# Layer 0 of a graph-attention stack: rows that travel by rank with all they need, wider MAX8 chunks, biases on TensorE

## The chip, the cores and the metric

The kernel runs on one core of a Trainium2 chip. The metric is the device time of one execution in microseconds; lower is better. It took 3183.84 us, the median of three runs (3183.69 to 3191.36).

## The reference

Four graph-attention layers run over 3327 nodes of 256 features and one adjacency matrix that they share. It is symmetric, with a full diagonal; a row has about 32 neighbours besides itself, and 52 at the most. Each layer adds its result to its input and normalises the row. Only layer 0 matters here:

```python
g_src = nodes @ W_src_w.T + W_src_b
g_tgt = nodes @ W_tgt_w.T + W_tgt_b
g = leaky_relu(g_src[:, None, :] + g_tgt[None, :, :], 0.2)
score = einsum('ijc,c->ij', g, a_w)
score = where(adj_mat != 0, score, -inf)
x = layernorm(x + softmax(score, axis=1) @ g_tgt)
```

The leaky ReLU stands inside the sum over features, so a score needs work on all 256 features of each pair. With about 1% of the pairs present, the kernel does it for the neighbours alone.

## The kernel before

Rows lie in 26 tiles of 128 (the last has 127). `sparse0` computes layer 0; the rest, `layers`, computes layers 1 to 3 with dense masks. At the very end one number, `lost`, says whether the sparse way dropped a neighbour; then `dense0` and the layers would run again.

The tiles form three sets of 5, 9 and 12 (`SETS`). For each tile `neighbours` (on VectorE, DVE) does the following:

- It loads the tile's adjacency rows in two halves of 1664 columns (`adj_i`, two buffers, SP's queue) and turns each entry into a column number or zero (`num`, L417).
- MAX8 takes the eight largest numbers of each chunk of `CHUNK` columns (L436). The first three of each chunk, and the eight largest of all the others (L445), go into `few`.
- Seven rounds of MAX8 and MATCH_REPLACE over `few` (L448, L450) give a sorted list of up to `KMAX` = 56 neighbours, `found`.
- The list, the row's own number and a mark for the diagonal form the row's `payload`. The number of neighbours gives a sort key; `key_rows` (TensorE) and L490 turn the keys of the set into ranks (`ranks_i`, L494).

Rows of a set are then processed in the order of their ranks, those with most neighbours first, so that a tile of 128 rows gathers only as many columns of lists as its first row needs (`LEVELS`). For this the rows must be rearranged. `write_list` (GpSimd, POOL) scatters a tile's payloads by rank into `lists_d`; `read_lists` loads the whole set's lists in rank order (`lst`).

Beside this, for every tile, `targets` projects the rows by `w_tgt` on TensorE, adds the bias on DVE (L358), copies one column on ACT (L359) and writes the row to `table_d` and to `own_d`. `sources` does the same with `w_src`, adds and negates on DVE (L374) and writes to `own_d`. So a row of `own_d` (`OWN` = 772 words) holds the row's negated source, its input x (copied straight from DRAM on POOL's queue) and its target.

The main loop walks over 126 parts of up to eight list columns. For a part q:

- `gather(q + 4)` issues one indirect DMA on POOL per list column (`g`, L544): 128 rows of `table_d`. Before a tile's first part it gathers the tile's rows of `own_d` by their own numbers (`own_of`, L536).
- `score(q)` (DVE) takes the larger of target and negated source (L563) and sums it, weighted by `a_w` (L569).
- After a tile's last part, `combine` takes the softmax; ACT scales the gathered rows (L650) and TensorE adds them up (L653). `add_input` (DVE) adds x, and `put_back` (POOL) scatters the result to `sums_d`.

The steps of `neighbours` for sets two and three are spread over the parts by a fixed plan (`owed`, `goal`), so DVE alternates between scores of one set and lists of the next. List writes wait in `between` and are issued one per two gathers. The order on PE, DVE, ACT and POOL in `sparse0` is the order of the program; SP's order is made by the framework's scheduler. Waits on a queue hold everything that stands behind them.

Of the kernel before, what the change touches and what calls it, by code (L numbers as in the profile page):

```python
# [8 lines left out]
F32 = mybir.dt.float32  # L9
BF16 = mybir.dt.bfloat16  # L10
I32 = mybir.dt.int32
U32 = mybir.dt.uint32
U16 = mybir.dt.uint16
AF = mybir.ActivationFunctionType
ALU = mybir.AluOpType
AX = mybir.AxisListType
# [3 lines left out]
P = 128  # L20
# [7 lines left out]
KMAX = 56  # L28
CHUNK = 64
FIRST = 3  # L30


SETS = (5, 9, 12)
# [6 lines left out]
FAR = 1e6  # L40

ROW = 260
OWN = 772


@with_exitstack
def gat_stack(
# [54 lines left out]
    table_d = dram.tile([nt * P, ROW], F32, name="table_d")  # L102
# [161 lines left out]

    def sparse0(lost):
        GROUP, TURNS, LEAD = 8, 11, 4
        starts = [sum(SETS[:s]) for s in range(len(SETS))]
        with ExitStack() as s0:
# [14 lines left out]
            w_tgt = const0.tile([P, kc, dim + 1], F32, name="w_tgt0")  # L283
            nc.sync.dma_start(w_tgt[:, :, :dim], w_tgt_t.rearrange("(c p) f -> p c f", p=P))
            a_row = load_row(const0, a_w, "a_row")
            bt_row = load_row(const0, b_tgt, "bt_row")
            w_src = const0.tile([P, kc, dim], F32, name="w_src0")
            nc.scalar.dma_start(w_src, w_src_t.rearrange("(c p) f -> p c f", p=P))
            bs_row = load_row(const0, b_src, "bs_row")
# [12 lines left out]
            for lo, hi in halves:  # L302
                hi = -(-hi // P) * P
                rev_i = io0.tile([P, nt * P // 2], I32, tag="adj_i", name="rev_i")
                nc.gpsimd.iota(
                    rev_i[:, : hi - lo], pattern=[[-1, hi - lo]], base=n - lo,
                    channel_multiplier=0,
                )
                nc.vector.tensor_copy(rev[:, lo:hi], rev_i[:, : hi - lo])
# [14 lines left out]
            for s, size in enumerate(SETS):  # L324
                lo, hi = starts[s] * P, min(n, (starts[s] + size) * P)
                own_d.append(dram.tile([size * P, OWN], F32, name=f"own{s}_d"))
                copy_rows(nc.gpsimd, own_d[s][: hi - lo, dim : 2 * dim], x[lo:hi, :])
# [12 lines left out]
            def project(p, xt, pn, weight):  # L340
                for k in range(kc):
                    nc.tensor.matmul(
                        p[:pn, : weight.shape[2]], xt[:, k, :pn], weight[:, k, :],
                        start=(k == 0), stop=(k == kc - 1),
                    )

            def targets(it):

                xt, pn = columns_of(it)
                row = io0.tile([P, ROW], F32, tag="row", name="row", bufs=3)  # L350
                nc.vector.memset(row[:, dim:], 0.0)
                if pn < P:
                    nc.vector.memset(row[:, :dim], 0.0)
                    nc.vector.memset(row[:, dim : dim + 1], -FAR)
                pt = ps0.tile([P, BANK], F32, tag="acc", name="pt")
                project(pt, xt, pn, w_tgt)
                yield
                nc.vector.tensor_add(row[:pn, :dim], pt[:pn, :dim], bt_row[:pn])  # L358
                nc.scalar.copy(row[:pn, dim : dim + 1], pt[:pn, dim : dim + 1])  # L359
                nc.scalar.dma_start(table_d[it * P : (it + 1) * P, :], row)  # L360
                nc.scalar.dma_start(own_rows(it)[:, 2 * dim :], row)
                yield

            def sources(it):

                xt, pn = columns_of(it)
                pss = ps0.tile([P, BANK], F32, tag="ps", name="pss", bufs=1)
                project(pss, xt, pn, w_src)
                yield
                minus = io0.tile([P, dim], F32, tag="minus", name="minus")  # L370
                if pn < P:
                    nc.vector.memset(minus, 0.0)
                    nc.scalar.dma_start(own_rows(it)[pn:, dim : 2 * dim], minus[pn:])
                nc.vector.scalar_tensor_tensor(  # L374
                    minus[:pn], pss[:pn, :dim], -1.0, bs_row[:pn],
                    op0=ALU.mult, op1=ALU.subtract,
                )
                nc.scalar.dma_start(own_rows(it)[:, :dim], minus)
                yield

            lists_d = [
                dram.tile([size * P, KMAX + 2], U32, name=f"lists{s}_d")
# [5 lines left out]

            len_c = nt * P // CHUNK

            def neighbours(s):
# [6 lines left out]
                payloads = []  # L398
                of_rows = iter(())
                for t in range(size):  # L400
# [7 lines left out]
                    for b, (lo, hi) in enumerate(halves):  # L408
# [12 lines left out]
                        if lo <= it * P < hi:  # L421

                            at0 = it * P - lo
                            own_v = v[:, at0 : at0 + P]
                            junk = io0.tile([P, P], F32, tag="junk", name="junk")
                            nc.vector.scalar_tensor_tensor(
                                junk, own_v, -1.0, ident, op0=ALU.mult, op1=ALU.mult,
                                accum_out=sums[:, 2:3],
                            )
                            nc.vector.tensor_mul(own_v, own_v, off_diag)  # L430
                        chunks = padded // CHUNK
                        for c in range(chunks):
                            if c == chunks // 2:
                                next(of_rows if b else before, None)
                                yield
                            nc.vector.max(  # L436
                                cand[:, lo // CHUNK + c, :], v[:, c * CHUNK : (c + 1) * CHUNK]
                            )
                        yield
                    few = io0.tile([P, FIRST * len_c + 8], F32, tag="few", name="few")  # L440
# [4 lines left out]
                    nc.vector.max(few[:, FIRST * len_c :], cand[:, :, FIRST:])  # L445
                    found = io0.tile([P, KMAX], F32, tag="found", name="found")
                    for r in range(0, KMAX, 8):
# [11 lines left out]
                    payload = io0.tile([P, KMAX + 2], U32, tag=f"pay{t}", name="payload", bufs=1)  # L459
                    nc.vector.tensor_scalar(  # L460
                        payload[:, :KMAX], found, -1.0, float(n), op0=ALU.mult, op1=ALU.add
# [5 lines left out]
                    payloads.append(payload)  # L467
# [27 lines left out]
                placed[s] = ranks_i, payloads  # L495
# [5 lines left out]
            def write_list(s, t):  # L501
                ranks_i, payloads = placed[s]
                nc.gpsimd.indirect_dma_start(
                    out=lists_d[s][:, :],
                    out_offset=bass.IndirectOffsetOnAxis(ap=ranks_i[:, t : t + 1], axis=0),
                    in_=payloads[t][:, :], in_offset=None,
                )

            def read_lists(s):
                lst = io0.tile([P, max(SETS), KMAX + 2], U32, tag="lst", name="lst")  # L510
                nc.gpsimd.dma_start(
                    lst[:, : SETS[s], :], lists_d[s].rearrange("(t p) k -> p t k", p=P)
# [17 lines left out]
            def gather(q):  # L530
                (s, t), k0, k1 = parts[q]
                if k0 == 0:
# [3 lines left out]
                    nc.gpsimd.indirect_dma_start(  # L536
                        out=own[:, :], out_offset=None, in_=own_d[s][:, :],
                        in_offset=bass.IndirectOffsetOnAxis(ap=lst[:, KMAX : KMAX + 1], axis=0),
                    )
# [40 lines left out]
            def score(q):  # L580
# [6 lines left out]
                if k0 == 0:  # L587
                    sc = entry["sc"] = io0.tile([P, KMAX + 1], F32, tag="sc", name="sc", bufs=3)
                    if kt < KMAX:
                        at = nt + starts[s] + t  # L590
                        nc.vector.tensor_scalar(
                            lost[:, at : at + 1], entry["lst"][:, kt : kt + 1], float(n), None,
                            op0=ALU.is_lt,
# [206 lines left out]


# [44 lines left out]
            read_lists(0)  # L846

# [823 lines left out]
```

The softmax here doesn't subtract the row's maximum and nothing guards it: scores larger than these inputs give would overflow.

## Time and profile before

| | us |
|---|---|
| median of three runs | 3183.84 |
| profiled execution | 3182.83 |
| its span | 3181.0 |
| first adjacency tile arrives on DVE | 27.2 |
| ranks of the first set | 142.8 |
| first gather | 168.0 |
| last gather | 1514.9 |
| last result of layer 0 put back | 1540.8 |

In the profile, PE is TensorE, PEld its weight load, DVE VectorE, ACT ScalarE, POOL GpSimd and SP SyncE; L544 is line 544 of the kernel. A group of instructions is shown with its count, its busy time, the mean of one in ns, and the idle time of its engine just ahead of it. DVE is busy for 2316.7 us of the span (73%), PE for 2170.4 (68%), POOL for 1042.3 (33%), ACT for 734.7 (23%); these are means over stages with different limits. A line of a timeline gives start, duration, engine and instruction, and in brackets how long the engine stood idle ahead of it and what released it.

### The profile page before, as it was taken

To read this page: it belongs to the slowest core of one execution; us is meant where nothing else is said; L and a number is where in the kernel's file an instruction comes from. 1 tells how busy PE (TensorE), PEld (TensorE's weight loads), DVE (VectorE), ACT (ScalarE), POOL (GpSimd) and SP (SyncE) were. 2 spreads that over 40 slices of the span, in tenths; PEclk is the share of its full clock that TensorE was granted. 3 is DMA by queue.
4 is the path that set the end of the run, shared out by engine and by line. 5 is a ranking of instruction groups with operands and counts; after the bars stand their busy time and mean duration, and the time that the engine had idled before them with its cause. 6 is when DMAs were issued, how large, how long until landed. Compare 5 with 4: busy or idle time off the path is not lost.

```text
span 3181.0 us, 44618 instructions
## 1 busy us (share of the span) xinstructions
PE 2170.4 (68%) x15572; PEld 1239.5 (39%) x15572; DVE 2316.7 (73%) x6592; ACT 734.7 (23%) x2068; POOL 1042.3 (33%) x1056
## 2 busy tenths in 40 slices
PE   4204324335352445443689999999999999999996
PEld 2102112112121222221468888885444445444332
DVE  6879999999976655555425552107888898899997
ACT  0003222324331434433234431120111110110110
POOL 0077747677767777777100000000000000000000
PEclk6556666667676677666799999999999999999998
DMA  7556536655434544444657663332212212212211
GB/s 208 156 138 175 154 99 164 172 152 163 123 83 111 136 109 120 117 118 114 190 145 216 200 189 91 109 104 82 65 47 70 67 49 68 67 48 57 57 47 46
DMA packets 177752, 367.93 MB, mean 116 GB/s; under 512 B 34340, under 2 KB 123236, under 8 KB 176494
## 3 DMA queue, kind: packets, MB, share of 16 engines
q1 hardware_dynamic: 95798, 171.81, 19.3%
q0 software_dynamic: 51424, 157.02, 18.9%
q10 hardware_dynamic: 30296, 36.15, 3.2%
q8 instruction: 125, 2.05, 0.3%
q14 instruction: 109, 0.89, 0.1%
HBM read 322.84 MB, written 45.43 MB: 116 GB/s over the span
## 4 chain that ended last, share of the span: by engine, by line
PE 45%; DVE 4%; DMA 1%; issue 0%; ACT 0%; POOL 0%; ACTq 0%; SPq 0%; DVEq 0%; POOLq 0%
PE acc L1326 17%; PE acc L1279 15%; PE acc L1334 8%; DVE e L1195 3%; PE misc L1125 3%; DMA at_i<-in_adj_t_dram 1%; DMA at<-at_d 1%; PE misc L1222 0%; PE misc L1408 0%; PE misc L1369 0%; DVE h L246 0%; DVE stats L1486 0%; DVE h L1484 0%; DVE h L1299 0%; DVE both L1481 0%
## 5 line engine op out<-in xcount | busy, mean ns | idle before, releaser
L544 POOL DMA_INDIRECT g<-table_d,lst x923 | 914.5, 991 | 296.4 <-issue 270.4
L1195 DVE SCALAR_TENSOR_TENSOR e<-rate,feat,at 128x896 f32<-128x896 f32 (+4 forms) x832 | 843.9, 1079 | 80.6 <-PE acc L1334 70.0
L653 PE MATMUL acc<-g,ident 128*128 128x512 f32 (+1 forms) x934 | 460.1, 651 | 414.3 <-ACT g L650 405.2
L1326 PE MATMUL acc<-e,feat 128*32 128x384 f32 (+2 forms) x6656 | 689.0, 516 | 4.8 <-DVE e L1195 2.1
L653 PEld LDWEIGHTS acc<-g,ident 128*128 128x128 f32 x934 | 195.7, 214 | 651.8 <-ACT g L650 426.5
L563 DVE TENSOR_TENSOR y<-g,both 128x1024 f32<-128x1024 f32 (+2 forms) x240 | 275.7, 1173 | 203.6 <-DMA g<-table_d,lst 194.6
L1326 PEld LDWEIGHTS acc<-e,feat 128*32 128x32 f32 x6656 | 259.2, 110 | 343.2 <-issue 233.8
L1334 PE MATMUL acc<-e,feat 128*32 128x384 f32 (+3 forms) x3328 | 375.6, 513 | 0.0
L650 ACT ACTIVATE g<-g,w 128x256 f32<-128x256 f32 x923 | 370.6, 493 | 0.0
L569 DVE SCALAR_TENSOR_TENSOR y<-y,both 128x256 f32<-128x256 f32 x923 | 324.6, 416 | 0.0
L1279 PE MATMUL acc<-feat,e 128*128 128x257 f32 (+2 forms) x1352 | 306.6, 383 | 23.6 <-DMA at_i<-in_adj_t_dram 14.4
L1279 PEld LDWEIGHTS acc<-feat,e 128*128 128x128 f32 (+2 forms) x1352 | 255.4, 191 | 63.7 <-issue 15.4
L240 POOL TENSOR_TENSOR rstds<-rstds,minus_half 128x7 f32<-128x7 f32 (+1 forms) x12 | 19.8, 1650 | 752.8 <-DVE rstds L239 752.8
L1279 PE MATMUL acc<-feat,at 128*128 128x257 bf16 (+2 forms) x2028 | 236.4, 273 | 7.0 <-DMA at<-at_d 6.7
L481 PE MATMUL key_rows<-key_diag,ones 128*128 128x128 f32 x52 | 17.7, 439 | 311.7 <-DVE key_diag L480 257.7
L1279 PEld LDWEIGHTS <-at 128*128 128x128 bf16 (+2 forms) x2028 | 197.7, 99 | 40.3 <-DMA at<-at_d 4.8
L1334 PEld LDWEIGHTS acc<-e,feat 128*32 128x32 f32 (+1 forms) x3328 | 139.3, 110 | 155.3 <-issue 131.8
L1195 DVE SCALAR_TENSOR_TENSOR e<-rate,feat,at_i 128x896 f32<-128x896 f32 (+2 forms) x104 | 111.1, 1079 | 94.9 <-ACT feat L1133 54.6
L436 DVE MAX8 cand<-num 128x8 f32<-128x64 uint16 x1352 | 179.0, 209 | 1.0
L1175 POOL DMA_DIRECT2D rate3b_d<-rate_rows x4 | 2.1, 520 | 467.2 <-ACT rate_rows L1174 467.2
L481 PEld LDWEIGHTS key_rows<-key_diag,ones 128*128 128x128 f32 x52 | 12.2, 278 | 324.9 <-DVE key_diag L480 214.3
L559 ACT COPY both<-own_of 128x256 f32<-128x256 f32 x26 | 9.7, 375 | 500.5 <-DMA own_of<-own_d,lst 367.4
(174 smaller groups left out, 1766.0 us busy)
## 6 DMA issues: line engine op xcount, KB each, us to landing
at<-at_d SPq DMA_DIRECT2D x150, 224.0 KB, 2.5
at_i<-in_adj_t_dram SPq DMA_DIRECT2D x50, 448.0 KB, 4.1
adj_i<-in_adj_dram SPq DMA_DIRECT2D x25, 832.0 KB, 4.6
adj_i<-in_adj_dram SPq DMA_DIRECT2D x25, 831.5 KB, 4.9
g<-table_d,lst POOLq DMA_INDIRECT x923, 2.8
at<-at_d SPq DMA_DIRECT2D x75, 192.0 KB, 2.4
at<-at_d SPq DMA_DIRECT2D x75, 191.8 KB, 2.4
at_d<-at ACTq DMA_DIRECT2D x50, 224.0 KB, 4.2
```

Source lines behind the costliest of these rows:

```text
L436: nc.vector.max(cand[:, lo // CHUNK + c, :], v[:, c * CHUNK : (c + 1) * CHUNK])
L481: nc.tensor.matmul(key_rows[:, t * P : (t + 1) * P], ones, key_diag, start=True, stop=True)
L544: nc.gpsimd.indirect_dma_start(out=g[:, k - k0, :], out_offset=None, in_=table_d[:, :], in_offset=bass.IndirectOffsetOnAxis(ap=entry["lst" ...
L563: nc.vector.tensor_tensor(y, rows, minus_src[:, None, :].to_broadcast([P, m, dim]), op=ALU.max)
L569: nc.vector.scalar_tensor_tensor(y, y, 1.0, a, op0=ALU.mult, op1=ALU.mult, accum_out=sc)
L650: nc.scalar.activation(rows, rows, AF.Copy, scale=w[:, k : k + 1])
L653: nc.tensor.matmul(dst, ident, rows, start=start, stop=stop)
L1125: nc.tensor.matmul(pacc[:pn, : dim + self.extra], ht[:, k, :pn], self.weight[:, k, :], start=(k == 0), stop=(k == kc - 1),)
L1195: nc.vector.scalar_tensor_tensor(e[:pn, : c1 - c0], self.rate[b][:pn, h_of, : c1 - c0], q, at[:pn, : c1 - c0], op0=ALU.max, op1=ALU.mult,)
L1279: nc.tensor.matmul(accs[s][:pn, : dim + 1], a[:pj, s * P : s * P + pn], f[:pj, : dim + 1], start=(j == 0 and part == 0), stop=(j == nt - 1 ...
L1326: nc.tensor.matmul(accs[x][p][q : q + 32, : hi - lo], f[:pj, at0 : at0 + 32], es[at0 // hd][:pj, lo:hi], start=(j == 0), stop=(j == nt - 1),)
L1334: nc.tensor.matmul(accs[x][pairs][h_of * 32 : (h_of + 1) * 32, : hi - lo], f[:pj, dim + h_of : dim + h_of + 1].to_broadcast([pj, 32]), es[ ...
```

## The change

- **Rows by rank.** A row of `own_d` gets its payload as well (`RANKED` = 830 words). `write_list` loads a tile's rows from `own_d` on SP (`rows`, two buffers) and scatters them whole by rank into `ranked_d`. `gather` then reads a tile's own rows as one plain block on SP; the indirect gather by row number is gone. `read_lists` reads the last 58 words of the ranked rows. The payload goes out by a DMA on SP, and needs three buffers instead of one per tile.
- **Chunks.** `CHUNK` grows from 64 to 104. A chunk consists of two runs of 52 columns, one in each half of the 1664. One more entry of `few`, `lack`, holds the sum of all numbers less the sum of those chosen, so that a single dropped neighbour comes back. Columns count upwards from `BASE`, and row 0 of `table_d` stands for "none".
- **Biases.** They are added on TensorE by a matmul with a row of ones; ACT copies the projections out of PSUM.
- **Copies of x.** Those of sets two and three are issued on SP instead of POOL; the program has them after the first `read_lists`.

```diff
-CHUNK = 64
+CHUNK = 104
+BASE = 4096
+RANKED = OWN + KMAX + 2
@@ sparse0
-                    rev_i[:, : hi - lo], pattern=[[-1, hi - lo]], base=n - lo,
+                    rev_i[:, : hi - lo], pattern=[[1, hi - lo]], base=BASE + lo,
...
-                copy_rows(nc.gpsimd, own_d[s][: hi - lo, dim : 2 * dim], x[lo:hi, :])
+                if s == 0:
+                    copy_rows(nc.gpsimd, own_d[s][: hi - lo, dim : 2 * dim], x[lo:hi, :])
...
+                if bias is not None:
+                    nc.tensor.matmul(
+                        p[:pn, : weight.shape[2]], ones[:1, :pn], bias, start=False, stop=True
+                    )
@@ targets
-                project(pt, xt, pn, w_tgt)
+                project(pt, xt, pn, w_tgt, bt_row)
                 yield
-                nc.vector.tensor_add(row[:pn, :dim], pt[:pn, :dim], bt_row[:pn])
-                nc.scalar.copy(row[:pn, dim : dim + 1], pt[:pn, dim : dim + 1])
...
+                nc.scalar.copy(row[:pn], pt[:pn, :ROW])
@@ sources
-                nc.vector.scalar_tensor_tensor(
-                    minus[:pn], pss[:pn, :dim], -1.0, bs_row[:pn],
-                    op0=ALU.mult, op1=ALU.subtract,
-                )
+                nc.scalar.mul(minus[:pn], pss[:pn, :dim], -1.0)
@@ neighbours
+                        spread_v = v[:, :padded].rearrange(
+                            "p (x c i) -> p c x i", x=2, i=CHUNK // 2
+                        )
...
-                                cand[:, lo // CHUNK + c, :], v[:, c * CHUNK : (c + 1) * CHUNK]
+                                cand[:, lo // CHUNK + c, :], spread_v[:, c, :, :]
...
+                    nc.vector.tensor_reduce(
+                        sums[:, 3:4], few[:, : FIRST * len_c + 8], axis=AX.X, op=ALU.add, negate=True
+                    )
+                    lack = few[:, FIRST * len_c + 8 :]
+                    nc.vector.tensor_reduce(lack, sums, axis=AX.X, op=ALU.add)
+                    nc.vector.tensor_scalar_min(lack, lack, float(BASE + n - 1))
...
-                    payload = io0.tile([P, KMAX + 2], U32, tag=f"pay{t}", name="payload", bufs=1)
+                    payload = io0.tile([P, KMAX + 2], U32, tag="pay", name="payload", bufs=3)
...
-                    payloads.append(payload)
+                    nc.sync.dma_start(own_rows(it)[:, OWN:], payload.bitcast(F32))
@@ write_list
-                ranks_i, payloads = placed[s]
+                rows = io0.tile([P, RANKED], F32, tag="rows", name="rows", bufs=2)
+                nc.sync.dma_start(rows, own_rows(starts[s] + t))
                 nc.gpsimd.indirect_dma_start(
-                    out=lists_d[s][:, :],
-                    out_offset=bass.IndirectOffsetOnAxis(ap=ranks_i[:, t : t + 1], axis=0),
-                    in_=payloads[t][:, :], in_offset=None,
+                    out=ranked_d[s][:, :],
+                    out_offset=bass.IndirectOffsetOnAxis(ap=placed[s][:, t : t + 1], axis=0),
+                    in_=rows[:, :], in_offset=None,
                 )
@@ gather
-                    nc.gpsimd.indirect_dma_start(
-                        out=own[:, :], out_offset=None, in_=own_d[s][:, :],
-                        in_offset=bass.IndirectOffsetOnAxis(ap=lst[:, KMAX : KMAX + 1], axis=0),
-                    )
+                    nc.sync.dma_start(own, ranked_d[s][t * P : (t + 1) * P, :OWN])
@@ after read_lists(0)
+            for s in range(1, len(SETS)):
+                lo, hi = starts[s] * P, min(n, (starts[s] + SETS[s]) * P)
+                copy_rows(nc.sync, own_d[s][: hi - lo, dim : 2 * dim], x[lo:hi, :])
```

## The prediction

> **What bounds the kernel now.** I read the 40 slices first, then the busy times by stage, then who waits for whom on GpSimd (POOL), then the few POOL steps between the last rank and the first gather.
>
> ```profile
> DVE  6879999999976655555425552107888898899997
> ...
> POOL 0077747677767777777100000000000000000000
> ...
> L544 POOL DMA_INDIRECT g<-table_d,lst x923 | 914.5, 991 | 296.4 <-issue 270.4
> ...
> L436 DVE MAX8 cand<-num 128x8 f32<-128x64 uint16 x1352 | 179.0, 209 | 1.0
> ```
>
> POOL works only in slices 3 to 20: that is layer 0. Its last step is at 1541 us, and all that comes later is the other layers, which the change does not touch; I let them move along unchanged. A gather (L544) costs POOL about 0.95 us and 0.30 us of issue, so 1.25 us from start to start.
>
> ```profile
> 27.00:143.00 116.00, 48.15 (x122) 32.50 (x122) 101.32 (x519) 3.98 (x25) 0.00 (x0) 0.60 0.59 172
> 171.50:432.90 261.40, 77.01 (x167) 37.67 (x168) 247.89 (x1114) 54.10 (x139) 174.75 (x167) 0.60 0.56 151
> 432.90:905.40 472.50, 180.17 (x402) 86.45 (x400) 459.41 (x1986) 132.75 (x341) 348.83 (x340) 0.67 0.53 146
> 905.40:1515.00 609.60, 269.88 (x600) 124.97 (x600) 351.07 (x1315) 226.57 (x616) 462.15 (x486) 0.70 0.45 115
> ```
>
> Columns after the length: PE, weight load, DVE, ACT, POOL busy with counts, granted clock, DMA share, GB/s. The cuts are my choice: first adjacency landed, first scores, ranks of the second set (432.9), ranks of the third (905.4), last gather. I call the stages prologue, A, B, C. With 0.30 us added per POOL instruction, POOL is occupied 225 of 261 us in A, 451 of 472 in B, 608 of 610 in C. DVE is 95% and 97% busy in A and B, 58% in C. So DVE sets the prologue, A and B; POOL sets C, and in B it has only 22 us to spare.
>
> ```profile
> POOL lists_d L503 <- DVE lost L591: 24.9, 1, 24.9
> POOL lists_d L503 <- DVE inv L676: 10.2, 1, 10.2
> DVE row L358 <- PE pt L342: 10.4, 4, 2.6
> ```
>
> The first two are POOL held at the first list write of sets two and three until DVE has the ranks: these two waits tie POOL to DVE at the ends of A and B. The third is DVE waiting in the prologue to add a bias.
>
> ```profile
> 143.26 2.43 POOL L503 DMA_INDIRECT lists_d<-payload,ranks_i  x1 [135.68 <-DVE ranks_i L494]
> ...
> 160.85 0.96 POOL L503 DMA_INDIRECT lists_d<-payload,ranks_i  x1 [1.97 <-DMA lists_d<-payload,ranks_i]
> 163.34 0.93 POOL L511 DMA_DIRECT2D lst<-lists_d  x1 [1.53 <-DMA lists_d<-payload,ranks_i]
> 166.71 0.99 POOL L536 DMA_INDIRECT own_of<-own_d,lst  x1 [2.44 <-DMA lst<-lists_d]
> 168.01 0.95 POOL L544 DMA_INDIRECT g<-table_d,lst  x1 [0.30 <-issue]
> ```
>
> Five list writes, each held until the one before has landed, take 143.3 to 163.3: 20 us with nothing beside them. Landing times decide the new version of this:
>
> ```profile
> at_i<-in_adj_t_dram SPq DMA_DIRECT2D x50, 448.0 KB, 4.1
> ...
> lists_d<-payload,ranks_i POOLq DMA_INDIRECT x26, 2.2
> own_of<-own_d,lst POOLq DMA_INDIRECT x26, 4.2
> ```
>
> **DVE work of a row tile.** Rates: one more column costs 1.04 ns (L563: 1213 ns for 1024 columns, 411 for 256). MAX8 on 64 columns takes 179.0/1352 = 132 ns; on 104, 132+40x1.04 = 174 ns. Per tile 52x132 = 6.88 us become 32x174 = 5.57: 1.31 saved. The candidates shrink from 164 to 105 columns: 7 MAX8 and 6 MATCH_REPLACE lose 61 ns each, 0.80. The MAX8 over the rest goes from 260 to 160 columns, 0.10; the copy into few, 0.06. Added: a sum over 104 columns (L455 takes 205 ns for 56, so 255), a sum over 4 (L458, 157), a minimum (L464's kind, 144): 0.56. Net 1.71 us saved. The source bias (L374, 406 ns, 0.35 from start to start) leaves DVE too: 2.06 per tile in the loop.
>
> No row shows a MAX8 over two runs. Lower bound of the break: nothing. The Trainium skill ("Vector Engine (DVE) Microarchitecture Reference", Measured stream behaviour on trn2) says a port keeps full rate over runs of at least two adjacent 4-byte words, whatever hops lie between; runs of 52 uint16 satisfy that, and no run here shows it. Upper bound: a second instruction's fixed part, 132-64x1.04 = 65 ns, 2.1 us per tile, which eats the whole DVE gain. I take nothing, the skill being the only near evidence.
>
> **Prologue.** Five tiles: 5x1.71 = 8.6. The target bias goes to TensorE and the copy to ACT: 25 additions of 0.33 us from start to start, 8.3, and the 10.4 us of waiting for PE. Four source biases, 1.4. Ranks come about 28 us earlier. TensorE gets a one-row matmul per projection (PE is under half busy), ACT copies of 0.38 us for 0.16 and 26 multiplications of 0.38 (ACT is 3% busy here, 28% in B): hidden by that idle time; without it, 16 us on ACT. The copies of x for sets two and three go from POOL's queue to SP's; in the changed order they stand ahead of the first adjacency load. That load now takes 14.5 us beside the same bytes; alone it would take about 5. Between 9 us gained and 10 lost (the copies landed in 13.0 and 18.9 us) I take 0, since the bytes are the same.
>
> **The start.** Each of the five scatters now carries 128x3320 B = 425 KB instead of 30 KB, and is fed by a row load on SP. Nearest row for its landing: own_of, 395 KB, 4.2 us, against 2.2 for a list: +2.0 each, +10 us in all. The Trainium skill speaks against this change here: "DMA: Bandwidth & Descriptors", Anatomy of one DMA, puts a fixed 2.0 us of mostly completion latency on every DMA and only bytes/436 GB/s on top. By it the scatter costs just 0.9 us more (+4.5 in all), but each new link (payload to own_d, own_d to rows, rows to ranked_d) pays its fixed part. I use the trace. Two loads stand ahead of the ranks; those of tiles three to five wait for the scatter two earlier (two buffers) and take about 4.2 us (at_i, 4.1) while the next scatter flies. The payload write (about 3.4 us as own_d<-minus) ends before the ranks. The own gather leaves POOL, -1.3. Start in sum: -28+10-1.3 = -19.
>
> **A and B.** MAX8 counts give the tiles: 416 in A (8 tiles), 624 in B (12). A: 8x2.06 and 0.7 for the tile begun before: -17; POOL's slack of 36 us covers it. B: 12x2.06 = -24.7. POOL's floor there: 22 us of slack and 8 own gathers x1.25 = 10, less 5 for scatters, 27 us. So DVE still ends B, narrowly: -24. If that cover were gone B would give about -17.
>
> **C.** POOL loses 13 own gathers x1.25 = -16. It keeps 12 scatters. Two buffers mean that a scatter waits for the one two earlier to land (4.4, estimated from own_of), a load's issue and landing (0.4+4.2): 9 us per two, against 7.6 now (list writes stand 3.8 apart). So 0.75 us each, 10 of them: +7.5. By the skill's figure (3.0 per transfer) the cycle would be 6.5 and cost nothing; bounds 0 and 15. Net -9.
>
> Own loads, row loads and payload writes add 78 issues of about 0.4 us to SP, which idles. The added 22 MB meet a DMA share of 0.5; the gathers are four groups ahead, some 40 us. If that lead shrank, DVE would wait for g in B as it does in C.
>
> Sum: -19-17-24-9 = -69. Against the profiled execution's 3182.8 (span 3181.0 and 1.8 around it): 3114; the median lies 1.0 higher, so 3115.
>
> **Rivals.** (1) The prologue does not follow DVE: the first adjacency load lands later behind the copies, or SP's one queue (targets' columns, adjacency, payloads, rows) feeds it late. For: SP issues in order, and its xt loads already held it 12 to 14 us at a time. Against: DVE waited for adjacency only once. Price: 10 us for the copies and 10 of the 28 lost: 3135.
> (2) The scatters are cheaper and the coupling in A and B loosens: no stalls in C (-7.5), scatter +0.9 instead of 2.0 (-5.5), first adjacency earlier (-9): 3093.
> (3) The two-run MAX8 pays its break: 25 tiles x2.1 = +52: 3167.
> (4) Slower: row loads stand in SP's order behind adjacency loads that wait for DVE to free a buffer. 24 halves in B's 472 us are one release per 20 us. If each load waited so, a two-buffer cycle would take 20 us, a scatter 10 instead of 3.8: (10-4.5)x21 = +115, or 3230. It turns the sign when the cycle exceeds about 9+2x69/21 = 15.6 us. Against: in the changed order only the fifth and the eighth load of set two have an adjacency load directly ahead, and ten of set three stand together.
> (5) The change does not do what it says: a chunk with more than eight neighbours would lose more than the one that `lack` brings back, and the dense version would follow. Counting the reference's adjacency: in chunks of 104 in two runs none exceeds eight, and a row's candidates beyond each chunk's first three are at most seven, with room for eight; one run of 104 columns has one chunk with eleven. Nothing for it.
>
> **How the numbers follow.** Main case 0.64 (3115, by itself 3095 to 3135); (1) 0.15; (2) 0.08; (3) 0.05; (4) 0.05; gains that vanish in several places, 0.03. The range 3085 to 3150 leaves out (3), (4) and the tails. Within 0.3% (9.5 us, about what a measurement of this kernel tells from nothing): 0.03. Slower 0.05. Faster 0.92, with (3), whose 3167 lies 16 us under.
>
> **What would show it.** MAX8 at about 174 ns each and 832 of them; no L358 counterpart on DVE; ranks near 115 us and first gather near 149; second ranks near 397, third near 845; DVE still over 93% in A and B; no own gather on POOL; scatters landing in 4 to 5 us; gathers ending near 1446. Wrong: ranks after 125, scatters more than 6 us apart in C, MAX8 over 200 ns, or POOL waiting for rows.

## The result, and the profile after

| kernel | median (us) | shown runs | ratio to before | profiled run, its span |
|---|---|---|---|---|
| before | 3187.35 | 3183.69 to 3191.36 | 1 | 3182.83, 3181.0 |
| changed | 3145.56 | 3143.38 to 3153.67 | 0.9873, 95% [0.9849, 0.9897] | 3143.38, 3141.5 |

The change takes 42 us by the medians of four runs each (3183.84 above is that of three) and 39.5 by the two spans. I had forecast 69. The time is inside the range and the sign is right, but two fifths of the expected gain are missing, and this is what the experiments are about.

Two of the chips that the experiments ran on took 3589 and 3625 us for the kernel before, with engines standing between instructions all through the gather loop, and from runs on these only the time up to the first gather is read, which came out the same for the one kernel that ran on both kinds (ranks at 128.9 and 129.0, first gather at 153.7 and 153.8).

First the slices and two groups of the page of the changed kernel.

```profile
DVE  6579999999955655554345542108888899899997
...
POOL 0077747777767777776000000000000000000000
...
L564 POOL DMA_INDIRECT g<-table_d,lst x923 | 918.5, 995 | 289.4 <-issue 264.5
...
L449 DVE MAX8 cand<-num 128x8 f32<-128x104 uint16 x832 | 145.6, 251 | 1.0
```

POOL is done with layer 0 a slice earlier. The gathers are as many and as long as before. MAX8 is there 832 times, and 145.6/832 = 175 ns each: the forecast was 174, with nothing for the break between the two runs.

Then the windows, cut at the same events: first adjacency work, ranks, first gather, second ranks, third ranks, last gather.

```profile
27.80:131.10 103.30, 89.71 (x175) 47.80 (x174) 83.55 (x377) 10.58 (x28) 0.00 (x0) 1.00 0.68 206
131.10:164.30 33.20, 0.00 (x0) 0.00 (x0) 10.40 (x43) 1.06 (x3) 7.23 (x6) 1.00 0.60 198
164.30:415.60 251.30, 82.25 (x182) 40.18 (x183) 231.88 (x969) 56.09 (x145) 178.66 (x166) 0.83 0.59 158
415.60:868.20 452.60, 184.97 (x428) 88.54 (x426) 436.63 (x1770) 137.71 (x355) 338.08 (x332) 0.68 0.60 170
868.20:1475.00 606.80, 266.41 (x600) 123.33 (x600) 350.54 (x1315) 226.39 (x616) 452.43 (x474) 0.71 0.50 130
```

| step | forecast (us) | before to after | measured (us) |
|---|---|---|---|
| ranks of set one | -28 | 142.8 to 131.1 | -11.7 |
| ranks to first gather | +8.7 | 25.2 to 33.2 | +8.0 |
| A | -17 | 264.8 to 251.3 | -13.5 |
| B | -24 | 472.6 to 452.6 | -20.0 |
| C, to the last gather | -9 | 609.5 to 605.9 | -3.6 |
| sum | -69 | 1514.9 to 1474.1 | -40.8 |

What follows the last gather is 1666 us before and 1667 after: the other layers moved along, as assumed. More than half of what is missing, 16 of 28 us, is missing in the prologue. The first line above says where to look: VectorE (the third busy number) is busy 83.6 of 103.3 us, after 101 of 116 before, and TensorE (the first) went from 48.2 to 89.7. VectorE now has a wait of its own (engine, line waited for, total, times, longest):

```profile
DVE row L367 <- DMA own_d<-row: 11.8, 1, 11.8
```

L367 is the memset of the row buffer of the last target tile, the only one with fewer than 128 nodes. VectorE runs its list in order, so the adjacency work behind that memset stood until a row buffer came back from the chain projection, ACT copy, write.

### The profile page after: what moved, and what is told of

Read it like the earlier page. It is cut to its first block, busy times and chain, and to the rows that moved or that the text cites. A ratio compares the mean times of both kernels' runs of the same rounds, so it can differ in the third digit from the quotient of the medians.

```text
span 3141.5 us, 44429 instructions
## 1 busy us (share of the span) xinstructions
PE 2232.4 (71%) x15676; PEld 1260.5 (40%) x15676; DVE 2259.5 (72%) x6075; ACT 749.8 (24%) x2094; POOL 1017.8 (32%) x1027
## 4 chain that ended last, share of the span: by engine, by line
PE 45%; DVE 4%; DMA 1%; issue 1%; ACT 0%; POOL 0%; ACTq 0%; SPq 0%; DVEq 0%; POOLq 0%
PE acc L1354 17%; PE acc L1307 15%; PE acc L1362 8%; DVE e L1223 3%; PE misc L1153 3%; DMA at<-at_d 1%; DMA at_i<-in_adj_t_dram 1%; PE misc L1250 0%; PE misc L1436 0%; PE misc L1397 0%; DVE stats L1514 0%; DVE h L250 0%; DVE h L1512 0%; DVE h L1327 0%; DVE both L1509 0%
## 5 line engine op out<-in xcount | busy, mean ns | idle before, releaser
L1307 PE MATMUL acc<-feat,e 128*128 128x257 f32 (+2 forms) x1352 | 307.2, 383 | 22.9 <-DMA feat<-feats_d 13.5
L659 ACT ACTIVATE w<-sc,top 128x57 f32<-128x57 f32 (+15 forms) x26 | 8.5, 325 | 681.4 <-DVE top L656 639.3
L449 DVE MAX8 cand<-num 128x8 f32<-128x104 uint16 x832 | 145.6, 251 | 1.0
```

The costliest lines, as they stand in the source:

```text
L449: nc.vector.max(cand[:, lo // CHUNK + c, :], spread_v[:, c, :, :])
L1307: nc.tensor.matmul(accs[s][:pn, : dim + 1], a[:pj, s * P : s * P + pn], f[:pj, : dim + 1], start=(j == 0 and part == 0), stop=(j == nt - 1 ...
```

## Experiments

**Who sets the ranks now?** Theory PE: the bias matmul has one row, but costs TensorE as much as a matmul over 128 rows, so TensorE ends the prologue. Rivals: the one memset is the cause by itself; or TensorE's additions are hidden, as I had forecast.

Memset moved:

```diff
-                    nc.vector.memset(row, 0.0)
+                    nc.gpsimd.memset(row, 0.0)
```

> The changed kernel with one instruction moved: the memset of the last target tile's row (the only tile with fewer than 128 nodes) goes from VectorE to GpSimd. In the changed kernel VectorE stands 11.8 us behind it, until a row buffer comes free. Rival M (that wait is the cause by itself): ranks of set one 11 to 12 us earlier, near 119.5, total -11. Theory PE (TensorE is back to back until 122.9 us, the wait is a consequence): VectorE waits for TensorE elsewhere, at the sources or at the transposes of the ranks; ranks at most 4 us earlier, 127 to 131, total 0 to -4.

Measured: ranks at 129.2 (-1.9), last gather 1477.1, total 3145.69, ratio 0.9864 [0.9848, 0.9881]. The 11.8 us of waiting were a consequence and not the cause: with the memset away, VectorE is done only 1.9 us sooner (3.3 from its first MAX8 on, which came 1.4 later), and waits elsewhere (5.5 us for an adjacency load, and 4.6 for TensorE's `key_rows`, 0.9 in the changed kernel).

Bias made cheap for TensorE, at the same place (three bf16 rows whose sum is the fp32 row, made once at the start):

```diff
-    p[:pn, : weight.shape[2]], ones[:1, :pn], bias, start=False, stop=True
+    p[:pn, : weight.shape[2]], ones_b[:3, :pn], bias, start=False, stop=True
```

> The changed kernel with the bias of each projection as three bf16 rows that sum to the fp32 row, one bf16 matmul over three rows instead of one fp32 matmul over one row; else as changed. Theory PE: the bias step falls from two passes to one of a quarter or so of the time, some 0.9 us less in each of the about 33 projections before the ranks, so up to 28 us less TensorE time; the ranks come 8 to 13 us earlier (118 to 123), where VectorE takes over as the limit. Rival H (hidden): ranks unchanged within 2 us. Total by PE theory -8 to -14, by H 0.

Measured: ranks at 117.3 (-13.8), first gather 152.1, last gather 1461.7, total 3128.03, ratio 0.9814 [0.9798, 0.9830]. The ranks come even a little earlier than theory PE had it. VectorE is busy 83.4 of the 89.3 us before them: it limits again, so the 13.8 us are not all that TensorE was relieved of. The groups of TensorE before the ranks, shapes kept apart, first the changed kernel, then this one (count, busy time and mean ns at the end of the line, then idle time):

```profile
L353 PE MATMUL pt<-w_tgt,xt 128*128 128x260 f32 x100 | 51.9, 675 | 16.4 <-DVE w_tgt L304 7.2 <-ACT row L371 5.9 <-DMA xt<-in_x_t_dram 3.3
L358 PE MATMUL pt<-bt_row,ones 1*128 1x260 f32 x50 | 30.8, 716 | 0.0
...
L358 PE MATMUL pss<-bs_row,ones 1*128 1x256 f32 x12 | 7.3, 710 | 0.0
```

```profile
L373 PE MATMUL pt<-w_tgt,xt 128*128 128x260 f32 x100 | 38.1, 519 | 26.0 <-DMA xt<-in_x_t_dram 12.9 <-DVE w_tgt L324 12.2 <-ACT row L391 0.7
...
L378 PE MATMUL pt<-parts_b,ones_b 3*128 3x260 bf16 x25 | 7.8, 312 | 0.0
L378 PE MATMUL pss<-parts_b,ones_b 3*128 3x256 bf16 x6 | 1.9, 315 | 0.0
```

The one-row matmul over 260 columns has two fp32 passes (one for each record of the trace) like any other, and its mean pass, 716 ns, is not shorter than that of a pass over 128 rows, 675 ns. It takes 30.8+7.3 us, and with bf16 7.8+1.9. The passes over 128 rows got shorter as well, 51.9 to 38.1 us; the last section comes back to that. The rows of the timeline show it without means: in the changed kernel projections follow each other without a gap.

```profile
61.02 2.10 PE L353 MATMUL pt<-w_tgt,xt 128*128 128x260 f32 x4
63.05 1.23 PE L358 MATMUL pt<-bt_row,ones 1*128 1x260 f32 x2
64.21 2.10 PE L353 MATMUL pt<-w_tgt,xt 128*128 128x260 f32 x4
66.25 1.23 PE L358 MATMUL pt<-bt_row,ones 1*128 1x260 f32 x2
```

From start to start a projection takes 3.2 us, of which the bias is 64.21-63.05 = 1.16.

Biases back on VectorE, the rest as changed:

```diff
-                project(pt, xt, pn, w_tgt, bt_row)
+                project(pt, xt, pn, w_tgt)
-                nc.scalar.copy(row[:pn], pt[:pn, :ROW])
+                nc.vector.tensor_add(row[:pn], pt[:pn, :ROW], bt_wide[:pn])
...
-                nc.scalar.mul(minus[:pn], pss[:pn, :dim], -1.0)
+                nc.vector.scalar_tensor_tensor(
+                    minus[:pn], pss[:pn, :dim], -1.0, bs_wide[:pn],
+                    op0=ALU.mult, op1=ALU.subtract)
```

> The changed kernel with both layer-0 biases back on VectorE (no one-row matmul, no ACT copy or multiplication), all else as changed. Theory PE (the one-row bias matmul costs TensorE a full pass, 1.16 us a projection, so that TensorE and not VectorE ends the prologue): the about 33 projections of the prologue lose some 38 us of TensorE time and VectorE gets about 10 us of additions back, so the ranks of set one stay where they are or come earlier, 125 to 133 us, although VectorE has more work. Rival H (the biases on TensorE are hidden, the prologue misses its forecast for another reason): VectorE's 9.7 us more come on top, ranks near 141. In the loop both say the same: VectorE gets 0.35 us a tile and 20 tiles back in A and B, +4 to +7 us. Total against the changed kernel: PE theory 0 to +8, rival +14 to +18.

Measured: ranks at 137.1, first gather 171.8, last gather 1485.6, total 3153.72, ratio 0.9895 [0.9878, 0.9911]. The ranks lie between what the two theories expected. TensorE is relieved (busy 45 of 109 us), but VectorE gets more than its own additions back:

```profile
DVE row L373 <- PE pt L355: 11.3, 5, 2.6
```

That is the wait of before, 10.4 us there. So the biases cost VectorE about 20 us in the prologue, as forecast, and moving them as this change does brings 6 (4.8 from the first MAX8 on, at 31.6 here and at 30.4 in the changed kernel), since TensorE takes the rest. This run gives VectorE's gain from the chunks too, with the biases where they were. Its windows A and B:

```profile
171.80:425.40 253.60, 75.33 (x169) 37.19 (x170) 234.93 (x978) 53.99 (x138) 174.54 (x166) 0.61 0.59 156
425.40:881.80 456.40, 179.23 (x401) 85.61 (x399) 440.86 (x1781) 132.64 (x341) 341.40 (x332) 0.68 0.60 169
```

VectorE is busy 234.9 us in A instead of 247.8, in B 440.9 instead of 459.5, so 1.6 and 1.55 us less a tile.

**The chunks alone** (biases and transfer by rank both undone):

> The changed kernel with the transfer by rank and the move of the biases both undone, so that only the chunks of 104 columns (with the zero row, the list by columns plus one, and the sum that brings one lost candidate back) remain. My forecast's price for the chunks: 1.71 us a tile, 8.6 us before the ranks, 14 in A, 20.5 in B, together -43 against the kernel before, or 3145. If the parts add up: what the biases on TensorE bring (1 us at the ranks to 10 us in all by the run with biases back on VectorE) is lost against the run with the list scatter alone. Rival: the chunks bring less than 1.71 us a tile, total above 3155.

> The chunks of 104 alone, again on a chip where the loop is not disturbed. Known from the first run: ranks at 134.1 us, 8.7 before those of the kernel before (my price was 8.6). Open is the loop. My price of 1.71 us a tile gives -14 in A and -20.5 in B, total -43, or 3143. Theory of the additive parts, from the runs since: VectorE's busy time falls by 1.55 to 1.6 a tile (biases on VectorE: 12.9 us less in A, 18.6 less in B than before), A 252 to 254, B 454 to 458, C 609 to 612 since the own gathers are back on GpSimd; last gather near 1477 to 1482, total 3145 to 3150.

Measured, for the time up to the first gather: ranks at 134.1 and 133.8, that is -8.7 and -9.0, where my price of five tiles at 1.71 us was 8.6. Of these, 1.2 and 1.6 are a first MAX8 that came earlier, at 28.6 and 28.2 for 29.8; from there to the ranks it took 105.5 and 105.6 us for 113.0, so the chunks brought 7.5, or 1.5 a tile. Their loop is not read (both ran on the chips with the longer loop), so the chunks' share of A and B is known by VectorE's busy time alone.

**What is the transfer by rank worth?** It is undone in this kernel; chunks and biases stay as changed:

```diff
-                rows = io0.tile([P, RANKED], F32, tag="rows", name="rows", bufs=2)
-                nc.sync.dma_start(rows, own_rows(starts[s] + t))
...
-                    in_=rows[:, :], in_offset=None,
+                    in_=payloads[t][:, :], in_offset=None,
...
-                    nc.sync.dma_start(own, ranked_d[s][t * P : (t + 1) * P, :OWN])
+                    nc.gpsimd.indirect_dma_start(
+                        out=own[:, :], out_offset=None, in_=own_d[s][:, :OWN],
+                        in_offset=bass.IndirectOffsetOnAxis(ap=lst[:, KMAX : KMAX + 1], axis=0))
```

> The changed kernel with the transfer by rank undone: only the list (30 KB) is scattered from SBUF, and a tile's own part is gathered indirectly on GpSimd as before the change; chunks of 104 and biases on TensorE stay. My forecast's prices: from the ranks to the first gather 25 us instead of 33.3 (-8), A unchanged, B about +4 (eight own gathers on GpSimd, which now ends B), C +9 (16 us of own gathers less 7.5 of scatter waits), total +4 against the changed kernel. Rival Z (in C the row transfer gives back in landing waits what it saves): C within 3 us of 605.9, so that undoing it gains the start's 8 us, total -5 to -8, and the transfer by rank is a loss.

> The same kernel as in the run of the list scatter (transfer by rank undone, chunks of 104 and biases on TensorE kept), on another chip: on the chip of the first run every kernel lost about 400 us between the first gather and the last, the kernel before as well, so that only its prologue and start could be read. Known from there: first gather 25 us after the ranks, 8 less than in the changed kernel. Open is the loop. My forecast's prices: B +4, C +9, total +4 against the changed kernel (3150, ratio 0.988). Rival Z (the landing waits of the row transfer eat in B and C what the own gathers saved): B and C within 3 us of 452.6 and 605.9, total -8 (3138, ratio 0.984).

Measured in the second: ranks 129.0, first gather 153.8, second ranks 404.6, third 857.5, last gather 1470.0, total 3138.84, ratio 0.9853 [0.9837, 0.9868]. Against the changed kernel: ranks -2.1, ranks to first gather 24.8 instead of 33.2, A and B the same within 0.5, C +6.6. By the last gather the transfer by rank costs 4.1 us; the totals point the same way with intervals that overlap, so it is nothing or a small loss. Neither theory had all of it: the start is as priced, C loses 6.6 where the forecast's price was 9, and B loses nothing, since VectorE sets it in both kernels (busy for 436.6 of 452.6 and of 452.9 us). The start, first changed and then undone:

```profile
131.54 2.43 POOL L525 DMA_INDIRECT ranked_d<-rows,ranks_i  x1 [126.20 <-DVE ranks_i L514]
139.79 0.98 POOL L525 DMA_INDIRECT ranked_d<-rows,ranks_i  x1 [5.82 <-DMA ranked_d<-rows,ranks_i]
144.28 0.96 POOL L525 DMA_INDIRECT ranked_d<-rows,ranks_i  x1 [3.51 <-DMA ranked_d<-rows,ranks_i]
151.39 0.96 POOL L525 DMA_INDIRECT ranked_d<-rows,ranks_i  x1 [6.16 <-DMA ranked_d<-rows,ranks_i]
155.60 0.96 POOL L525 DMA_INDIRECT ranked_d<-rows,ranks_i  x1 [3.25 <-DMA ranked_d<-rows,ranks_i]
...
164.34 0.99 POOL L564 DMA_INDIRECT g<-table_d,lst  x1 [4.42 <-DMA lst<-ranked_d]
```

```profile
129.44 2.43 POOL L524 DMA_INDIRECT lists_d<-payload,ranks_i  x1 [124.10 <-DVE ranks_i L515]
136.21 0.98 POOL L524 DMA_INDIRECT lists_d<-payload,ranks_i  x1 [4.34 <-DMA lists_d<-payload,ranks_i]
141.28 0.96 POOL L524 DMA_INDIRECT lists_d<-payload,ranks_i  x1 [4.09 <-DMA lists_d<-payload,ranks_i]
143.73 0.96 POOL L524 DMA_INDIRECT lists_d<-payload,ranks_i  x1 [1.49 <-DMA lists_d<-payload,ranks_i]
```

The bracket is the idle time ahead of the instruction and what ended it: in both the landing of the scatter before. In the changed kernel it is 3.3 or 3.5 us twice and about 6 twice. The long ones fall together with adjacency loads of 832 KB, which SP issued at 133.06 and 144.46. With the small scatters two such loads went out between 130.96 and 136.5, and the gaps are 4.3 and 4.1 then and 1.5 afterwards. So a wide scatter costs about 1.8 us more, with such a load beside it (6.0 for 4.2 in the mean) and without one (3.4 for 1.5).

**Buffers or landing?** One more row buffer, room for it taken from a buffer that VectorE alone uses:

```diff
-                rows = io0.tile([P, RANKED], F32, tag="rows", name="rows", bufs=2)
+                rows = io0.tile([P, RANKED], F32, tag="rows", name="rows", bufs=3)
```

> The changed kernel with three row buffers instead of two for the transfer by rank (room for it from one buffer less of num, which VectorE alone writes and reads). Theory R (a scatter's row load waits for the scatter two earlier to land, the 9 us cycle of my forecast): scatters in C closer together, GpSimd's waits at the scatters (42.6 us in 18 waits) fall by half, B and C -3 and -8, start -3 to -5, total -10 to -14. Rival W (each scatter waits for the landing of the one before it, since both write the same table; the load is there in time): waits unchanged, total within 3 us.

> Three row buffers, again on a chip where the loop is not disturbed. Known from the first run: the start does not gain (36 us from ranks to first gather, against 33). Theory R (two row buffers make the cycle): GpSimd's waits at the scatters in B and C (12.6 and 11.3 us) fall by half or more, last gather 8 to 12 us earlier. Theory W (each scatter waits for the one before it to land): waits within 3 us of these, last gather within 3 us of 1474, total within 4 us of 3145.6.

Measured: ranks at 131.5 and 131.1, first gather at 167.4 and 164.9: no gain. (In the first, one gap was 7.8 us.) The gaps between scatters in the second run:

```profile
139.65 0.98 POOL L525 DMA_INDIRECT ranked_d<-rows,ranks_i  x1 [5.69 <-DMA ranked_d<-rows,ranks_i]
143.88 0.96 POOL L525 DMA_INDIRECT ranked_d<-rows,ranks_i  x1 [3.25 <-DMA ranked_d<-rows,ranks_i]
151.07 0.96 POOL L525 DMA_INDIRECT ranked_d<-rows,ranks_i  x1 [6.23 <-DMA ranked_d<-rows,ranks_i]
154.57 0.96 POOL L525 DMA_INDIRECT ranked_d<-rows,ranks_i  x1 [2.54 <-DMA ranked_d<-rows,ranks_i]
```

They are those of two buffers within 0.7 us. In the start it is the landing that counts, not the buffers. Their loop is not read (both ran on the same two chips), but the changed kernel's own trace, read below for C, points the same way there.

**The first set by lists, the others by rank:**

> The changed kernel, with the transfer by rank for sets two and three alone; the first set's lists are scattered from SBUF (30 KB each) and its own parts gathered indirectly. Theory: the scatters of the first set have nothing beside them, so their longer landing and the row loads stand on the path: first gather 7 to 9 us earlier (155 to 157 with the ranks at 131), five own gathers of 1.25 us are covered by GpSimd's wait of 22.7 us at the second ranks, and total -6 to -9. Rival (the lateness is absorbed by VectorE's work in A, which goes on meanwhile): first gather earlier, but the second ranks stay at 415.6, total within 2 us.

Measured up to the first gather: ranks 129.2, first gather 153.9, so 24.7 us between them instead of 33.2. Whether A keeps these 8 us this run does not show. With the transfer undone for all sets, above, it does: from the first ranks to the second ranks that kernel took 275.6 us against 284.5.

**The copies of x.** They stand on SP ahead of the first adjacency load; I had costed that at nothing. Here they go out from ACT's queue after the first lists:

```diff
-                copy_rows(nc.sync, own_d[s][: hi - lo, dim : 2 * dim], x[lo:hi, :])
+                copy_rows(nc.scalar, own_d[s][: hi - lo, dim : 2 * dim], x[lo:hi, :])
```

> The changed kernel with the two copies of x for sets two and three issued from ACT's queue after the first lists are read, instead of from SP where they stand ahead of the first adjacency load. Theory X (these copies delay the first adjacency load and ACT's row writes): first adjacency work on VectorE at 14 to 18 us instead of 27.8; since TensorE then starts its projections earlier, too, ranks 6 to 12 us earlier (119 to 125). Rival B (what my forecast assumed: the same bytes have to move, the order does not matter): first adjacency within 3 us of 27.8, ranks within 2 us. Total by X -6 to -12, by B 0.

Measured: first MAX8 at 21.0 instead of 30.4, ranks at 121.7 (-9.4), but first gather 160.9 (-3.4), last gather 1470.9 (-3.2); total 3142.70, ratio 0.9862 [0.9845, 0.9878]. What was won at the ranks went again in the start, which took 39.2 us. ACT issued the copies at 114.3, ahead of the ranks, because nothing on its list held it back, and they were under way while the scatters were (kind, size, median us from issue to landing; then the second scatter, which GpSimd stood idle for 8.79 us ahead of):

```profile
own_d<-in_x_dram ACTq DMA_DIRECT2D x1, 1520.0 KB, 21.8
```

```profile
133.44 0.98 POOL L525 DMA_INDIRECT ranked_d<-rows,ranks_i  x1 [8.79 <-DMA ranked_d<-rows,ranks_i]
```

**Put together:** bf16 rows for the bias, the memset on GpSimd, the first set by lists, and the copies of x inside the gather loop, where neither the first adjacency load nor the first scatters stand behind them:

```diff
+                if q in (1, 2):
+                    lo, hi = starts[q] * P, min(n, (starts[q] + SETS[q]) * P)
+                    copy_rows(nc.scalar, own_d[q][: hi - lo, dim : 2 * dim], x[lo:hi, :])
```

> A version put together from the runs before: the changed kernel with the bias as three bf16 rows, the last row's memset on GpSimd, the first set's lists scattered from SBUF with own gathers (transfer by rank for sets two and three alone), and the copies of x for sets two and three issued from ACT's queue inside the gather loop, where neither the first adjacency load nor the first scatters stand behind them. Additive theory: first adjacency work at 18 to 21 us (-7 or so), ranks at 104 to 110 (VectorE alone limits the prologue now: 116 us of it before the change less 28), first gather 25 us later at 130 to 136, A, B and C as in the changed kernel; last gather 28 to 34 us earlier, total 3111 to 3117 (ratio 0.977). Rival: the parts share one bound (TensorE's projections); ranks not before 114, total above 3120.

Measured: total 3117.08 (3114.68 to 3119.93), at the upper edge of what was expected, ratio 0.9784 [0.9771, 0.9797]; the interval lies wholly below that of the change, 0.9849 to 0.9897. First MAX8 at 22.5, ranks 108.3, first gather 133.2, last gather 1450.6. The windows from the first MAX8 to the ranks, and A to C:

```profile
22.50:108.30 85.80, 55.31 (x150) 31.90 (x150) 80.59 (x370) 10.55 (x28) 0.32 (x1) 0.69 0.80 234
133.20:389.10 255.90, 75.07 (x175) 37.05 (x176) 232.28 (x970) 57.09 (x147) 178.46 (x170) 0.60 0.63 171
389.10:842.60 453.50, 178.70 (x414) 85.47 (x412) 436.66 (x1771) 137.75 (x355) 336.60 (x329) 0.69 0.60 169
842.60:1451.00 608.40, 269.22 (x600) 124.49 (x600) 350.48 (x1315) 226.41 (x616) 452.94 (x476) 0.70 0.50 130
```

VectorE is busy 80.6 of 85.8 us: it sets the prologue again. The parts add up to the ranks and the first gather as expected. A is 4.6 us longer than in the changed kernel and C 2 longer, which leaves 23.5 of the 31 us gained at the first gather. The 4.6 us lie at the very start of A: from the first gather to VectorE's first weighted sum 18.3 us go by, and in the changed kernel 13.2 (13.1 and 13.2 with the transfer undone and with the bf16 rows alone). ACT issues the copies of x from 137.3 on, and the gathers of these 18 us land after 6.0 us in the median (2.8 to 9.6), in the changed kernel after 2.8 (2.7 to 3.2). So by the traces it is the copies that make A longer; they were not tried there by themselves.

## Why the prediction was right or wrong

**Right: the work of a tile on VectorE.** MAX8 at 175 ns for 174. The chunks brought 1.5 us a tile in the prologue and 1.6 and 1.55 of busy time in A and B, for 1.71. Together with the source bias VectorE's busy time fell by 15.9 in A and 22.9 in B, for 16.5 and 24.7.

**Right: the start.** Ranks to first gather grew by 8.0 for 8.7, and undoing the transfer takes 8.4 off again. The median landing of a scatter by rank is 4.2 us, and the estimate from the trace was 4.4; by the Trainium skill's fit for a DMA of GpSimd's queue, 2.0 us and bytes over 436 GB/s ("DMA: Bandwidth & Descriptors", Anatomy of one DMA), I estimated 3.0. The fastest came near that, with 3.1; for the median, of scatters that other loads run beside, the trace decides against it. That two of the gaps would be long, beside adjacency loads, was not foreseen; with the small scatters two are long as well, so the difference came out right.

**Wrong: the prologue, at the words "hidden by that idle time".** The ranks at 131.1 are past the 125 that I had named as a sign of being wrong. The chunks came, 7.5 us for 8.6. Of the 20 us for the biases, the wait for TensorE with them, 5 came (134.1 to 129.0). With the transfer by rank the ranks are 2 later again (129.0 to 131.1), all of it ahead of the first MAX8 (28.2 and 30.4); why is open. I had counted the one-row matmul by its row and not by its columns, and had looked at TensorE's busy share as if free time at any place would serve. Each projection got longer by 1.16 us; with 32 projections ahead of the ranks (100 and 24 passes of full length at four a projection, and the last tile) that is 37 us. TensorE's busy time from the start to the ranks rose by 49.6, from 54.9 to 104.5; the rest is that its passes over 128 rows got longer too (last section). The wait of VectorE for a projection was in that very chain: to take VectorE out of it does not help where the chain itself becomes the longer one. The Trainium skill has a line that would have warned me ("TensorE: Matmul & The Clock Gate", Why this matters for your kernels): a single matmul over 32 rows takes the time of one over 128. This trace shows the same for one row, 716 ns a pass against 675. That this term failed and not the rest of the step is shown by the bf16 rows: with the bias step at a quarter of the time the ranks come at 117.3, close to the 115 of the forecast.

**Wrong in size: B and C.** I let VectorE end B, "narrowly", with 3 us of room for GpSimd. VectorE does still set the third ranks: in B its only wait that the trace names is 3.4 us for TensorE. Its busy time fell by 22.9, but the time between its instructions grew from 13.1 to 16.0 (why is open), so 20.0 came. GpSimd's room is gone: at the third ranks it used to wait 10.2 us for VectorE, and now it comes 1.2 us after them.

```profile
869.35 0.99 POOL L525 DMA_INDIRECT ranked_d<-rows,ranks_i  x1 [0.30 <-issue]
```

The ranks were there at 868.2. GpSimd's waits from the second ranks to the last gather that speak of scatters, first changed and then with the transfer undone:

```profile
POOL ranked_d L525 <- DMA ranked_d<-rows,ranks_i: 23.9, 14, 3.9
POOL ranked_d L525 <- DVE lost L611: 22.7, 1, 22.7
```

```profile
POOL lists_d L524 <- DVE lost L612: 17.7, 1, 17.7
POOL lists_d L524 <- DMA lists_d<-payload,ranks_i: 3.3, 2, 1.7
```

Of the 23.9 us 12.6 are in B, where I had 5, and 11.3 in C, where I had 7.5. Those of B used up GpSimd's room and little else, since the ranks would not have come sooner. Those of C count: 16 us of own gathers less 11.3, and about 1 for the late start, are 4, and 3.6 were measured for my 9.

I had let a scatter of C wait for its row load, and the load for the scatter two earlier. In the trace it waits for the scatter just ahead of it to land. The row loads issued at 888.9, 893.7 and 898.5 take 3.5 us in the median, so they are there some 2 us ahead of their scatters at 894.4, 898.8 and 903.8. That the size was near is luck. C's scatters stand 4.87 us apart and the small ones 4.05, in the kernel before too ((950.3-905.8)/11); I had 4.5, and had read 3.8 for the 4.05.

```profile
L525 POOL DMA_INDIRECT ranked_d<-rows,ranks_i x11: 990/990/992, 869.4 to 918.0; - x11
L524 POOL DMA_INDIRECT lists_d<-payload,ranks_i x12: 987/989/990, 859.6 to 904.1; - x12
```

**A** gave 13.5 of 17. VectorE's busy time accounts for 15.9; the time between its instructions grew from 17.0 to 19.4, as in B. Its first weighted sum comes 13.2 us after the first gather in both kernels, so the gathers are not the reason.

**The copies of x at nothing**: the sum was right and the reason half right. They delay the first adjacency work by 9.4 us, but moved behind it they take 6.0 of that from the start, where the bytes meet the scatters. In the gather loop they hold up neither of the two, but the first gathers, by 5 us.

**The rivals.** The first, a prologue that does not follow VectorE, came within 11 us in price (3135), but by TensorE and not by SP's queue. The measured 3145.56 lies outside the 3095 to 3135 of my main case; what holds it is the room that the range gave to this rival. Of the second (cheaper scatters) nothing was seen, their landing being 4.2 us for the assumed 4.2 to 4.4; nor of the third (a break in MAX8), 175 ns; nor of the fourth (row loads behind adjacency loads), where two scatters of C take 9.7 us, far from 15.6; nor of the fifth (the dense version follows), since what comes after the last gather is as long as before.

## What to carry to other kernels

Price a small matmul by its columns and its number of passes, not by its rows: here one row cost as much as 128 over the same 260 columns. Ask what one more of them does to the chain that already feeds the engine you want to relieve, and not whether the other engine has idle time on average. A wait of engine X for engine Y goes away only if Y's chain gets shorter; moving X's instruction onto Y's side can make it longer. A transfer that is made larger to save a later one is paid where it stands on the path: here the wide scatter costs 8 us at the start, where nothing hides it, and saves 7 in C, which speaks for the later sets alone.

## What the hardware showed that I had not expected

The same four fp32 passes of a projection took 1.91 to 2.10 us throughout the changed kernel's prologue, and in the bf16 version some took 1.14 and some 1.91:

```profile
64.87 1.91 PE L373 MATMUL pt<-w_tgt,xt 128*128 128x260 f32 x4
66.71 0.28 PE L378 MATMUL pt<-parts_b,ones_b 3*128 3x260 bf16 x1
66.92 1.14 PE L373 MATMUL pt<-w_tgt,xt 128*128 128x260 f32 x4
```

So did some in the kernel before:

```profile
60.95 1.14 PE L342 MATMUL pt<-w_tgt,xt 128*128 128x257 f32 x4 [1.87 <-ACT row L359]
```

All fourteen traces fall in two groups. In the eight with the one-row fp32 step (the changed kernel among them) not one of the 32 projections ahead of the ranks takes less than 1.91 us, although TensorE works there without a gap from 45 to 123 us in the changed kernel. In the six without it (the kernel before, biases on VectorE, the chunks alone twice, bf16 rows, put together) the shortest take 1.03 to 1.13 us. The bf16 version differs from the changed kernel in this step and in making its rows at the start, so it is the step that keeps the other passes long, and part of what the bf16 rows brought (51.9 to 38.1 us in the 100 passes of the target projections) is this, beside the cheaper step itself. Whether it is its single row, its type or its length was not separated. The granted clock does not explain it: it reads 1.00 in the prologues of all eight and 0.60 to 0.69 in the six, which is the wrong way round for these durations.
